# A four-layer graph network on one core: 48 tile turns per pair moved from TensorE to VectorE and DRAM

## The chip, the core and the metric

The kernel runs on one core of one Trainium2 chip. The metric is the device time of one launch in microseconds (us). Before the change the median of 3 runs is 3835.46 us (3834.73 to 3838.8); the profiled execution spans 3831.4 us. The engines that matter are TensorE (PE, with its weight loads shown apart as PEld), VectorE (DVE), ScalarE (ACT), GpSimd (POOL), and SyncE (SP), from whose single queue every transfer is issued.

## What is computed

64 graphs of 256 nodes with 256 features pass four layers. Every layer normalises its input, applies a relu, runs a graph operator and adds the result to `x`:

```
h = max(layernorm(x), 0)
layer 0: x += 8-head masked attention(h) @ Wo + bo
layer 1: x += elu(masked additive attention(h), softmax over the first node axis)
layer 2: x += gated graph network(h), 3 steps:
             m = h @ weight[i];  aggr = A^T m;  h = GRU(aggr, h)
layer 3: x += 4-head masked additive attention(h)
```

Everything is float32 but the masks.

## The kernel before, in words

**Tiling.** Two graphs make a pair: 512 tokens, four tiles of 128 tokens, in one SBUF tile of 128 partitions x 1024 floats. There are 32 pairs and every pair passes the four layers. A product on TensorE contracts over partitions, so a weight product needs the normalised tile with features on partitions: `hT`, which holds for each of two feature chunks `k` the 512 tokens side by side. The tile with tokens on partitions (`xn`, and `h` in layer 2) serves where the contraction is over nodes.

**Norm and turn.** `norm_relu_T` (L487) takes the statistics on VectorE (L494, L496), the reciprocal root on GpSimd (L504, L505), and normalises on VectorE (L526; in layer 2 on ScalarE with the relu, L521). Then TensorE turns the tile in 8 transposes of 128x128 (L541), two groups of four, each into one PSUM bank; ScalarE or VectorE evicts each bank, with the relu (L550, L551) or plain (`evict`, L315, L316).

**Layer 2.** Each of the first two GRU steps ends with the new state `u` with features on partitions. The next `messages` product (L914) needs it with tokens on partitions, so 8 further transposes (L1002) and two evictions turn it back. The gate products are at L933; the last step multiplies with the tokens on the output partitions (`tokens_mm`, L1022).

So there are six places per pair where TensorE turns a whole tile: four norms and two GRU steps, 48 transposes.

**The other way to turn, already there for the attention.** The softmax tiles of layers 0 and 3 are turned without TensorE (`turn_blocks`, L603): VectorE transposes 32x32 blocks in place (`STREAM_TRANSPOSE`, L606), one transfer writes the tile to a DRAM buffer `turn` (L608), four transfers of 32 partitions each read it back with the blocks exchanged (L611). This is done 12 times per pair. `by_dma` (L483) tells whether a norm or a GRU step is to be turned in this way too (`turn_chunks`, L621); before, it returns False always.

**Who uses a turned tile.** As stationary operand (through `chunk`, L558, or `chunk_of`, L900): the value product of layer 0 (L572), the products of layers 1 and 3 (L805, L1104), the messages (L914) and the last GRU step (L1022). As moving operand (through `wide`, L563): the query and key products (L679) and the gates (L933).

**Order.** Nothing is left to a scheduler at run time. `Plan` holds every task with an assumed duration, and `order` (L105) emits, one after another, the task that can begin first by these assumptions, with a priority from the pair's number, the length of the chain behind it and constants per layer and engine. Buffers are slots of a pool: a pair holds an `x` slot from its load to its store, working tiles are `w4` slots. Each engine then runs its instructions in this fixed order; an instruction that waits holds up all behind it on its engine, and on SyncE's queue.

Of the kernel before, what the change touches and what calls it, by code (L numbers as in the profile page):

```python
# [9 lines left out]
FP = mybir.dt.float32  # L10
# [12 lines left out]
class Buf:  # L23


    def __init__(self, tag, tiles):
        self.tag, self.tiles, self.slot, self.parts = tag, tiles, None, {}
        self.mixed = False

    def __call__(self):  # L30
# [7 lines left out]
class Plan:  # L38
# [11 lines left out]

    SPARE, GRAIN = 4, 0.01
    PERIOD, REST = 19.2988, 1.08912
    ON_PE = (170.952, 98.272, 202.056, -376.605)
    ON_SP = (-190.335, 1171.95, -256.975, 557.209)
    OTHERS = (254.735, -170.603, -1234.56, 1614.77)

    def __init__(self, slots, spare):
        self.slots, self.spare = slots, spare  # L60
# [120 lines left out]
def tile_adj_preln_d4(  # L181
# [38 lines left out]
    const = ctx.enter_context(tc.tile_pool(name="const", bufs=1))  # L220

    SLOTS = {
        "x": (5, [P, T * D], FP, 0),
        "w4": (29, [P, T * D], FP, 9),
        "f3": (2, [P, T, E3], FP, 0),
        "mask": (4, [P, T * N], BF, 1),
        "ps": (8, [P, 512], FP, 2),
# [254 lines left out]

    def by_dma(what, p):  # L483

        return False

    def norm_relu_T(xt, p, tokens=False):  # L487

        st, mv, rs = buf("st"), buf("mv"), buf("rs")
        for g in range(2):  # L490

            def stats(g=g):
                for t in (2 * g, 2 * g + 1):
# [12 lines left out]

        add((G, 1.4, rstd, True), reads=[mv], writes=[(rs, 0)])
        xn, mixed = w4(), by_dma(plan.layer, p)
        relu = tokens or mixed
        if relu:  # L510
            add(
                (V, 0.17, lambda: nc.vector.scalar_tensor_tensor(
                    rs()[:, 1, :], mv()[:, :, 0], -1.0, rs()[:, 0, :], ALU.mult, ALU.mult)),
                reads=[mv, (rs, 0)], writes=[(rs, 1)],
            )
        for g in range(2):

            def scaled(g=g):
                for t in (2 * g, 2 * g + 1):
                    if relu:  # L520
                        nc.scalar.activation(  # L521
                            tok(xn())[:, t, :], tok(xt())[:, t, :], AF.Relu,
                            bias=rs()[:, 1, t : t + 1], scale=rs()[:, 0, t : t + 1],
                        )
                    else:
                        nc.vector.tensor_scalar(  # L526
                            tok(xn())[:, t, :], tok(xt())[:, t, :], mv()[:, t, 0:1], rs()[:, 0, t : t + 1],
                            ALU.subtract, ALU.mult,
                        )

            add((A, 0.95, scaled) if relu else (V, 0.7, scaled, True), reads=[(xt, g), mv, rs], writes=[(xn, g)])
        hT = w4()
        if mixed:
            turn_chunks(xn, hT)
            return (at, hT, xn) if tokens else (at, hT)
        for k in range(2):
            ps = bank()

            def turn(k=k, ps=ps):
                for t in range(T):  # L540
                    nc.tensor.transpose(ps()[:, t * P : (t + 1) * P], tok(xn())[:, t, k * P : (k + 1) * P], ident)  # L541

            add((PE, 4 * TURN, turn), reads=[xn], writes=[ps], claims=[hT])
            dst = lambda k=k: tok(hT(), N2)[:, k, :]
            if tokens:
                add(evict(N2, dst, ps), reads=[ps], writes=[(hT, k)])
            else:
                add(
                    [
                        (A, act(N2), lambda dst=dst, ps=ps: nc.scalar.activation(dst(), ps(), AF.Relu)),  # L550
                        (V, dve(N2), lambda dst=dst, ps=ps: nc.vector.tensor_scalar_max(dst(), ps(), 0.0)),  # L551
                    ],
                    reads=[ps], writes=[(hT, k)],
                )
        return (at, hT, xn) if tokens else (at, hT)


    def chunk(hT, k, t):  # L558
        if hT.mixed:
            return hT().rearrange("p (n x) -> p x n", x=2 * T)[:, 2 * t + k]  # L560
        return tok(hT(), N2)[:, k, t * P : (t + 1) * P]

    def wide(hT, k):  # L563
        if hT.mixed:
            return hT().rearrange("p (n t k) -> p k t n", t=T, k=2)[:, k]
        return tok(tok(hT(), N2)[:, k, :], P)

    def graph_mm(ps, src, rhs, g, ):

# [33 lines left out]
    def turn_blocks(e, src, dst, eT):  # L603

        d = buf("turn")
        add((V, dve(T * N), lambda: nc.vector.transpose(dst(), src())), **e)  # L606
        e = e["writes"][0]
        add((SP, 0.6, lambda: nc.sync.dma_start(d(), e())), reads=[e], writes=[d], latency=4.6)  # L608
        for b in range(4):
            add(  # L610
                (SP, 0.55, lambda b=b: nc.sync.dma_start(  # L611
                    eT()[32 * b : 32 * b + 32, :].rearrange("p (a w) -> p a w", a=4),
                    d()[:, b * N : (b + 1) * N].rearrange("(a j) w -> j a w", a=4))),
                reads=[d], writes=[(eT, b)], latency=3.8,
            )

    def turn(e, eT):
        blocks = lambda: e().rearrange("p (r c i) -> p r c i", c=2, i=32)
        turn_blocks(dict(writes=[e]), blocks, blocks, eT)

    def turn_chunks(src, dst):  # L621

        e = w4()
        turn_blocks(
            dict(reads=[src], writes=[e]),
            lambda: src().rearrange("p (x b j) -> p b x j", b=4, j=32),
            lambda: e().rearrange("p (b i x) -> p b x i", b=4, i=32), dst,
        )
        dst.mixed = True

    def by_block(ap):
# [29 lines left out]
    def layer0(xt, p):  # L661
# [11 lines left out]
        for w, dst, nm in ((wq_sb, qT, "q"), (wk_sb, kT, "k")):  # L673
            for o in range(2):
                ps = bank()

                def product(w=w, o=o, ps=ps):
                    for k in range(2):
                        mm(ps(), w[:, k, o * P : (o + 1) * P], wide(hT, k), start=k == 0, stop=k == 1)  # L679

                add((PE, 1.72, product), reads=[hT, (QKV, int(w is wk_sb))], writes=[ps], claims=[dst])
                add(evict(N2, lambda dst=dst, o=o: tok(dst(), N2)[:, o, :], ps), reads=[ps], writes=[(dst, o)])
        for g in range(2):
            ps = bank()
            add((PE, 1.74, lambda ps=ps, g=g: graph_mm(ps, hT, wv_sb, g)), reads=[hT, (QKV, 2)], writes=[ps], claims=[v])
            add(evict(N2, lambda g=g: v()[:, g * N2 : (g + 1) * N2], ps), reads=[ps], writes=[(v, g)])


# [102 lines left out]
    def layer1(xt, p):  # L791
# [8 lines left out]
        for t in range(T):  # L800
# [6 lines left out]
            add((PE, 0.89, product), reads=[hT, W1], writes=[ps], claims=[wh, f12])  # L807
            add(
                (V, 0.07, lambda t=t, ps=ps: nc.vector.tensor_copy(f12()[:, :, t], ps()[:, D : D + 2])),
                reads=[ps], writes=[(f12, t)],  # L810
# [79 lines left out]
    def layer2(xt, p):  # L890
# [4 lines left out]
            reads=[hT], writes=[am],  # L895
        )
        at_o = lambda b, o: tok(b(), N2)[:, o, :]
        by_chunk = lambda b, o: tok(at_o(b, o), P)

        def chunk_of(h, t, o):  # L900
            if h.mixed:
# [2 lines left out]

        def messages(h):
            aT = w4()
            for o in range(2):
                ps = bank()

                def product(o=o, ps=ps):  # L910
                    for g in range(2):
                        for c in range(2):
                            t = 2 * g + c
                            mm(  # L914
                                ps()[:, g * N : (g + 1) * N], chunk_of(h, t, o), tok(am(), N)[:, t, :],
                                start=c == 0, stop=c == 1,
                            )

                add((PE, 1.73, product), reads=[h, am], writes=[ps], claims=[aT])
                add(evict(N2, lambda o=o: at_o(aT, o), ps), reads=[ps], writes=[(aT, o)])  # L920
            return aT

        for l in range(NL - 1):
            r, hn, u = w4(), w4(), w4()

            def gate(us, terms, c0, o, claims=()):
                ps = bank()
# [30 lines left out]
            for o in range(2):  # L958
# [8 lines left out]
                    writes=[(hn, o)],  # L967
                )
                add(
                    either(lambda eng, o=o, u=u, hT=hT, hn=hn: eng.tensor_sub(by_chunk(u, o), wide(hT, o), by_chunk(hn, o))),  # L970
                    reads=[(hT, o), (hn, o)], writes=[(u, o)],
                )

# [120 lines left out]
    def layer3(xt, p):  # L1094
# [4 lines left out]
        for t in range(T):  # L1099
# [6 lines left out]
            add((PE, 0.89, product), reads=[hT, W3], writes=[ps], claims=[f])  # L1106
# [125 lines left out]
```

## Time and profile before

| | before |
|---|---|
| time, median of 3 | 3835.46 us |
| span profiled, granted TensorE clock | 3831.4 us, 0.993 |
| tile turns on TensorE: L541, L1002 | 1024 and 512 instructions, 136.9 and 66.7 us busy |
| tile turns on VectorE: L606 | 384 instructions, 461.0 us busy |
| turn writes and reads by DMA | 384 of 512 KB, 1536 of 128 KB |
| DMA in all | 554.29 MB, mean 145 GB/s |

A profile row gives line, engine, operation, output<-inputs with buffer numbers left out, the shapes and the count; then the busy time of the group in us and the mean of one instruction in ns; then the idle time of the engine just before these instructions. One float32 product of the code is two PE records, except for a transpose, which is one. Matmuls overlap in the records, so a record's mean is longer than the distance from one start to the next; where the text speaks of a slot, it means this distance.

### The profile page before, as it was taken

What the parts mean: (1) busy time and instruction counts of PE and PEld (TensorE: products, weight loads), DVE (VectorE), ACT (ScalarE), POOL (GpSimd) and SP (SyncE); (2) the same over time, 40 slices, a digit from 0 to 9 for tenths busy, and PEclk for the clock granted to TensorE, in tenths of its full rate; (3) what the DMA queues carried; (4) which work ended last, traced back from release to release, by engine and by line L of the source; (5) the groups of instructions that cost most, each with busy time, mean ns of one, the idle gap of its engine ahead of it and who ended that gap; (6) DMA issues with size and microseconds to landing.
All of it is one profiled execution on the core that took longest, in us unless ns stands there. A gap on an engine that the chain in (4) does not pass through costs nothing. (4 is left out here: it accounts for less than half of the span.)

```text
span 3831.4 us, 55718 instructions
## 1 busy us (share of the span) xinstructions
PE 3771.1 (98%) x17072; PEld 2275.7 (59%) x17072; DVE 2909.2 (76%) x8279; ACT 2203.8 (58%) x6082; POOL 614.4 (16%) x595
## 2 busy tenths in 40 slices
PE   8999999999999999999999999999999999999995
PEld 5666556565666556565656565566666565655653
DVE  8796778778777788677787777786777787787655
ACT  6674456566555666555665556665456665466434
POOL 2001112111111111111111111111111111110111
PEclk9999999999999999999999999999999999999997
DMA  8354425553345544355533455442556334554224
GB/s 249 120 186 126 124 86 179 168 162 118 124 151 162 175 152 133 90 177 168 174 121 119 145 163 174 152 146 84 168 168 179 128 122 137 163 168 152 83 66 127
DMA packets 402202, 554.29 MB, mean 145 GB/s; under 512 B 40304, under 2 KB 340208, under 8 KB 401904
## 3 DMA queue, kind: packets, MB, share of 16 engines
q1 hardware_dynamic: 401904, 550.73, 46.7%
q8 instruction: 137, 2.24, 0.2%
q14 instruction: 161, 1.32, 0.1%
HBM read 332.15 MB, written 218.43 MB: 144 GB/s over the span
## 5 line engine op out<-in xcount | busy, mean ns | idle before, releaser
L655 ACT ACTIVATE w<-w,mx 128x256 f32<-128x256 f32 x1536 | 757.4, 497 | 36.7 <-DVE mx L647 36.6
L315 ACT COPY w<-ps 128x512 f32<-128x512 f32 (+1 forms) x632 | 360.8, 584 | 637.7 <-PE ps L914 165.9
L933 PE MATMUL ps<-w,giT 128*128 128x512 f32 x1536 | 712.6, 594 | 0.0
L933 PE MATMUL ps<-w,whhT 128*128 128x512 f32 x1536 | 707.9, 596 | 0.0
L933 PEld LDWEIGHTS ps<-w,giT 128*128 128x128 f32 x1536 | 288.1, 190 | 354.9 <-issue 339.0
L933 PEld LDWEIGHTS ps<-w,whhT 128*128 128x128 f32 x1536 | 283.7, 190 | 315.6 <-issue 288.2
L606 DVE STREAM_TRANSPOSE w<-w 128x1024 f32<-128x1024 f32 x384 | 461.0, 1223 | 10.3 <-ACT w L655 9.1
L647 DVE CUSTOM_DVE_ANT_0 w<-ps,mask 128x256 f32<-128x256 f32 x1024 | 368.6, 419 | 96.2 <-PE ps L699 95.0
L1022 PE MATMUL ps<-whhT,w 128*128 128x512 f32 (+1 forms) x1024 | 364.3, 489 | 0.0
L1022 PE MATMUL ps<-giT,w 128*128 128x256 f32 (+1 forms) x1024 | 359.6, 486 | 0.0
L914 PE MATMUL ps<-w,w 128*128 128x256 f32 x1536 | 355.8, 381 | 0.0
L970 POOL TENSOR_TENSOR w<-w,w 128x512 f32<-128x512 f32 x128 | 166.7, 1303 | 1114.7 <-ACT w L965 948.3
L914 PEld LDWEIGHTS ps<-w,w 128*128 128x128 f32 x1536 | 287.6, 190 | 52.3 <-issue 9.1
L655 ACT ACTIVATION_READ_ACCUMULATOR w<-w,mx 128x1 f32 x1536 | 292.2, 190 | 0.0
L1022 PEld LDWEIGHTS ps<-giT,w 128*128 128x128 f32 x1024 | 192.6, 190 | 142.0 <-issue 128.1
L1022 PEld LDWEIGHTS ps<-whhT,w 128*128 128x128 f32 x1024 | 186.9, 190 | 110.1 <-issue 96.5
L504 POOL TENSOR_SCALAR rs<-mv 128x4 f32<-128x4 f32 x128 | 37.4, 292 | 1336.9 <-DVE mv L496 1313.3
L945 ACT ACTIVATE w<-ps,brz 128x512 f32<-128x512 f32 x128 | 87.4, 683 | 239.1 <-PE ps L933 200.1
L1125 ACT ACTIVATE w<-w,f 128x256 f32<-128x256 f32 x512 | 215.4, 504 | 8.0 <-DMA w<-row 6.1
L730 DVE TENSOR_SCALAR w<-w,rz 128x256 f32<-128x256 f32 x688 | 202.4, 355 | 0.1
L494 DVE BATCH_NORM_STATS2 st<-x 128x6 f32<-128x256 f32 x512 | 189.3, 411 | 9.2 <-DMA x<-in_x_dram 7.2
L526 DVE TENSOR_SCALAR w<-x,mv,rs 128x256 f32<-128x256 f32 x384 | 155.3, 461 | 53.9 <-POOL rs L505 33.4
(119 smaller groups left out, 5750.0 us busy)
## 6 DMA issues: line engine op xcount, KB each, us to landing
turn<-w SPq DMA_DIRECT2D x384, 512.0 KB
w<-turn SPq DMA_DIRECT2D x1536, 128.0 KB
w<-in_adj_dram SPq DMA_DIRECT2D x128, 512.0 KB
w<-row SPq DMA_DIRECT2D x64, 512.0 KB
x<-in_x_dram SPq DMA_DIRECT2D x64, 256.0 KB
out_dram<-x SPq DMA_DIRECT2D x64, 256.0 KB
w<-row SPq DMA_DIRECT2D x32, 256.0 KB
w<-in_L_gnn_weight_dram SPq DMA_DIRECT2D x3, 256.0 KB
```

The costliest lines, as they stand in the source:

```text
L315: (A, act(n), lambda: nc.scalar.copy(dst(), src())),
L494: nc.vector.bn_stats(st()[:, t, :], tok(xt())[:, t, :])
L526: nc.vector.tensor_scalar(tok(xn())[:, t, :], tok(xt())[:, t, :], mv()[:, t, 0:1], rs()[:, 0, t : t + 1], ALU.subtract, ALU.mult,)
L606: add((V, dve(T * N), lambda: nc.vector.transpose(dst(), src())), **e)
L647: nc.vector.tensor_tensor_reduce(row, src, mask, scale, 3.0e38, ALU.add, ALU.min, mn)
L655: nc.scalar.activation(row, row, AF.Exp, bias=mn()[:, r : r + 1], scale=-1.0, accum_out=zs()[:, z0(r) : z0(r) + 1])
L730: op(row, row, rz()[:, r : r + 1])
L914: mm(ps()[:, g * N : (g + 1) * N], chunk_of(h, t, o), tok(am(), N)[:, t, :], start=c == 0, stop=c == 1,)
L933: mm(ps(), w[:, k, c0 : c0 + P], wide(src, k), start=n == 0, stop=n == 2 * len(terms) - 1)
L970: either(lambda eng, o=o, u=u, hT=hT, hn=hn: eng.tensor_sub(by_chunk(u, o), wide(hT, o), by_chunk(hn, o))),
L1022: mm(out, chunk(src, k, t), w[:, k, c0 : c0 + n], start=m == 0, stop=m == 2 * len(terms) - 1)
L1125: (A, act(N, 1), lambda t=t, g=g, h=h, e=e, r=r: nc.scalar.activation(rows_of(e())[:, r].rearrange("p b (c j) -> p c b j", c=2), sd[g]().r ...
```

## The change

The change takes tile turns off TensorE. `by_dma` becomes true for pairs 1 to 30; the first and the last pair turn on TensorE as before. In these 30 pairs all six turns go over VectorE and DRAM. For each turn the normalising runs on ScalarE with the relu (`relu` is true where `mixed` is), and the 8 transposes and 2 evictions are replaced by two block transposes of 512 columns each, one write of 512 KB and four reads of 128 KB.

A tile turned this way is not laid out by chunk and token. Its free axis is (node, chunk, tile of tokens): for a fixed node `n` lie 4 floats of chunk 0 and 4 floats of chunk 1 (of the four token tiles) side by side, 8 floats in all. A moving operand therefore reads runs of 4 floats with 4 skipped; a stationary operand, which needs 128 nodes of one token tile, reads single floats 8 apart. Products that take the tile as moving operand put their columns out by (node, tile), so the query and key evictions (`by_node`) sort them back on writing. In layer 2 the state stays in that order (`woven`): the messages are evicted into it, and the last step reads its stationary operands 4 floats apart.

`x` gets 6 slots for 5, so six pairs can be in flight, and `w4` 28 for 29. The constants of the planner's priorities are new, so the order of the whole program is another one.

```diff
-    SPARE, GRAIN = 4, 0.01
-    PERIOD, REST = 19.2988, 1.08912
+    SPARE, GRAIN = 4, 0.001
+    PERIOD, REST = 138.279, 1.02081
...
-        "x": (5, [P, T * D], FP, 0),
-        "w4": (29, [P, T * D], FP, 9),
+        "x": (6, [P, T * D], FP, 0),
+        "w4": (28, [P, T * D], FP, 9),
...
     def by_dma(what, p):
 
-        return False
+        return 0 < p < B // 2 - 1
...
         if hT.mixed:
-            return hT().rearrange("p (n x) -> p x n", x=2 * T)[:, 2 * t + k]
+            return hT().rearrange("p (n x) -> p x n", x=2 * T)[:, T * k + t]
+        if hT.woven:
+            return tok(hT(), N2)[:, k].rearrange("p (n t) -> p t n", t=T)[:, t]
         return tok(hT(), N2)[:, k, t * P : (t + 1) * P]
 
     def wide(hT, k):
+
         if hT.mixed:
-            return hT().rearrange("p (n t k) -> p k t n", t=T, k=2)[:, k]
-        return tok(tok(hT(), N2)[:, k, :], P)
+            return hT().rearrange("p (n k t) -> p k n t", k=2, t=T)[:, k]
+        return tok(hT(), N2)[:, k]
...
-    def turn_chunks(src, dst):
+        add((V, dve(T * N), lambda: nc.vector.transpose(blocks(), blocks())), writes=[e])
+        through_dram(e, eT)
+
+    def turn_chunks(src, order, dst):
 
         e = w4()
-        turn_blocks(
-            dict(reads=[src], writes=[e]),
-            lambda: src().rearrange("p (x b j) -> p b x j", b=4, j=32),
-            lambda: e().rearrange("p (b i x) -> p b x i", b=4, i=32), dst,
-        )
+
+        def blocks():
+            for k in range(2):
+                nc.vector.transpose(
+                    e().rearrange("p (b i k t) -> p k b t i", b=4, i=32, k=2)[:, k],
+                    src().rearrange(f"p {order} -> p k b t j", b=4, j=32, k=2)[:, k],
+                )
+
+        add((V, 2 * dve(N2), blocks), reads=[src], writes=[e])
+        through_dram(e, dst)
         dst.mixed = True
...
+                by_node = lambda ap, hT=hT: ap.rearrange("p (t n) -> p n t", t=T) if hT.mixed else ap
...
+        def messages_out(aT, o):
+            return at_o(aT, o).rearrange("p (n t) -> p t n", t=T) if woven else at_o(aT, o)
...
             if by_dma((2, l), p):
-                turn_chunks(u, h)
+                turn_chunks(u, "(k b j t)", h)
                 continue
```

More of the change, by code (lines that the diff above doesn't have):

```diff
@@ L27, in __init__ @@
         self.tag, self.tiles, self.slot, self.parts = tag, tiles, None, {}
+        self.woven = False
         self.mixed = False
@@ L48 @@
     SAME = {"PE": 0.0, "DVE": 0.1, "ACT": 0.1, "POOL": 0.1, "SP": 0.0}
-    SPARE, GRAIN = 4, 0.01
-    PERIOD, REST = 19.2988, 1.08912
-    ON_PE = (170.952, 98.272, 202.056, -376.605)
-    ON_SP = (-190.335, 1171.95, -256.975, 557.209)
-    OTHERS = (254.735, -170.603, -1234.56, 1614.77)
+    SPARE, GRAIN = 4, 0.001
+    PERIOD, REST = 138.279, 1.02081
+    ON_PE = (-212.355, -45.5106, 229.667, -1085.75)
+    ON_SP = (1007.6, 146.333, -62.4427, 928.914)
+    OTHERS = (294.968, 127.685, -2183.49, 1293.66)
     def __init__(self, slots, spare):
@@ L533, in norm_relu_T @@
         if mixed:
-            turn_chunks(xn, hT)
+            turn_chunks(xn, "(t k b j)", hT)
             return (at, hT, xn) if tokens else (at, hT)
@@ L601, in turned_keys, with through_dram @@
         return ap.rearrange("p (a t h c i) -> p h c t a i", a=4, t=2, h=2, c=2)[:, h, c]
-    def turn_blocks(e, src, dst, eT):
+    def through_dram(e, eT):
         d = buf("turn")
-        add((V, dve(T * N), lambda: nc.vector.transpose(dst(), src())), **e)
-        e = e["writes"][0]
         add((SP, 0.6, lambda: nc.sync.dma_start(d(), e())), reads=[e], writes=[d], latency=4.6)
@@ L618, in turn @@
         blocks = lambda: e().rearrange("p (r c i) -> p r c i", c=2, i=32)
-        turn_blocks(dict(writes=[e]), blocks, blocks, eT)
-    def turn_chunks(src, dst):
+        add((V, dve(T * N), lambda: nc.vector.transpose(blocks(), blocks())), writes=[e])
+        through_dram(e, eT)
+    def turn_chunks(src, order, dst):
         e = w4()
-        turn_blocks(
-            dict(reads=[src], writes=[e]),
-            lambda: src().rearrange("p (x b j) -> p b x j", b=4, j=32),
-            lambda: e().rearrange("p (b i x) -> p b x i", b=4, i=32), dst,
-        )
+        def blocks():
[6 more added lines that the diff above has]
+        through_dram(e, dst)
         dst.mixed = True
@@ L681, in layer0 @@
                 add((PE, 1.72, product), reads=[hT, (QKV, int(w is wk_sb))], writes=[ps], claims=[dst])
-                add(evict(N2, lambda dst=dst, o=o: tok(dst(), N2)[:, o, :], ps), reads=[ps], writes=[(dst, o)])
+                by_node = lambda ap, hT=hT: ap.rearrange("p (t n) -> p n t", t=T) if hT.mixed else ap
+                add(
+                    evict(
+                        N2, lambda dst=dst, o=o, f=by_node: f(tok(dst(), N2)[:, o, :]),
+                        lambda ps=ps, hT=hT: tok(ps(), T) if hT.mixed else ps(),
+                    ),
+                    reads=[ps], writes=[(dst, o)],
+                )
         for g in range(2):
             ps = bank()
-            add((PE, 1.74, lambda ps=ps, g=g: graph_mm(ps, hT, wv_sb, g)), reads=[hT, (QKV, 2)], writes=[ps], claims=[v])
+            add((PE, 2.0 if hT.mixed else 1.74, lambda ps=ps, g=g: graph_mm(ps, hT, wv_sb, g)), reads=[hT, (QKV, 2)], writes=[ps], claims=[v])
             add(evict(N2, lambda g=g: v()[:, g * N2 : (g + 1) * N2], ps), reads=[ps], writes=[(v, g)])
@@ L805, in product @@
                     mm(ps()[:, 0 : D + 2], chunk(hT, k, t), w1a[:, k, :], start=k == 0, stop=k == 1)
-            add((PE, 0.89, product), reads=[hT, W1], writes=[ps], claims=[wh, f12])
+            add((PE, 0.96 if hT.mixed else 0.89, product), reads=[hT, W1], writes=[ps], claims=[wh, f12])
             add(
@@ L897, in layer2 @@
         at_o = lambda b, o: tok(b(), N2)[:, o, :]
-        by_chunk = lambda b, o: tok(at_o(b, o), P)
+        woven = hT.mixed
+        def messages_out(aT, o):
+            return at_o(aT, o).rearrange("p (n t) -> p t n", t=T) if woven else at_o(aT, o)
         def chunk_of(h, t, o):
@@ L906, in messages @@
             aT = w4()
+            aT.woven = woven
             for o in range(2):
@@ L917, in product @@
                             )
-                add((PE, 1.73, product), reads=[h, am], writes=[ps], claims=[aT])
-                add(evict(N2, lambda o=o: at_o(aT, o), ps), reads=[ps], writes=[(aT, o)])
+                add((PE, 1.9 if h.mixed else 1.76, product), reads=[h, am], writes=[ps], claims=[aT])
+                add(
+                    evict(N2, lambda o=o: messages_out(aT, o), lambda ps=ps: tok(ps(), P) if woven else ps()),
+                    reads=[ps], writes=[(aT, o)],
+                )
             return aT
@@ L924, in layer2 @@
             r, hn, u = w4(), w4(), w4()
+            u.woven = woven
             def gate(us, terms, c0, o, claims=()):
@@ L969, in layer2 @@
                 add(
-                    either(lambda eng, o=o, u=u, hT=hT, hn=hn: eng.tensor_sub(by_chunk(u, o), wide(hT, o), by_chunk(hn, o))),
+                    either(lambda eng, o=o, u=u, hT=hT, hn=hn: eng.tensor_sub(
+                        *((tok(at_o(u, o), T), wide(hT, o), tok(at_o(hn, o), T)) if hT.mixed else (at_o(u, o), wide(hT, o), at_o(hn, o))))),
                     reads=[(hT, o), (hn, o)], writes=[(u, o)],
@@ L1104, in product @@
                     mm(ps()[:, 0:E3], chunk(hT, k, t), w3a[:, k, :], start=k == 0, stop=k == 1)
-            add((PE, 0.89, product), reads=[hT, W3], writes=[ps], claims=[f])
+            add((PE, 0.96 if hT.mixed else 0.9, product), reads=[hT, W3], writes=[ps], claims=[f])
             add(
```

## The prediction, made before the changed kernel was run

> **What bounds the kernel now.** I read the page's busy shares first, then the same by stretches of time, then the order of matmuls in a short window to get slots, then the groups.
>
> ```profile
> PE 3771.1 (98%) x17072; PEld 2275.7 (59%) x17072; DVE 2909.2 (76%) x8279; ACT 2203.8 (58%) x6082; POOL 614.4 (16%) x595
> ...
> DMA  8354425553345544355533455442556334554224
> ```
>
> TensorE is busy 98% of the span; no other engine is above 76%. A busy PE need not be a limit, so I ask where it is idle. The busy times by stretch (columns: stretch; length, then busy us and count of PE, PEld, DVE, ACT, POOL; clock, DMA share, GB/s):
>
> ```profile
> 0.00:40.00 40.00, 25.58 (x141) 17.82 (x142) 32.92 (x131) 19.68 (x56) 15.08 (x22) 0.92 0.87 281
> 40.00:115.00 75.00, 75.00 (x433) 45.74 (x433) 67.38 (x231) 53.10 (x171) 6.54 (x6) 0.98 0.78 229
> ...
> 1500.00:2000.00 500.00, 499.74 (x2225) 299.94 (x2224) 388.72 (x1116) 302.08 (x845) 79.14 (x76) 1.00 0.48 149
> ...
> 3500.00:3790.00 290.00, 278.88 (x1078) 165.06 (x1076) 184.33 (x416) 123.10 (x308) 45.56 (x39) 0.98 0.36 110
> 3790.00:3831.40 41.40, 9.33 (x40) 4.45 (x40) 14.34 (x42) 15.53 (x50) 0.00 (x0) 0.56 0.44 140
> ```
>
> In the middle PE never stops. All its idle time, 3831.4 - 3771.1 = 60 us, lies at the ends: 14.4 in the first 40 us, 43 after 3500. So from 115 to some 3600 us each nanosecond of PE taken away or added moves the end, as long as the others keep up. The order of matmuls in a window gives the slots:
>
> ```profile
> 1512.07 1.04 PE L1002 MATMUL ps<-ident,w 128*128 128x128 f32 x8
> 1512.95 1.89 PE L1022 MATMUL ps<-whhT,w 128*128 128x256 f32 x8
> 1514.67 3.62 PE L914 MATMUL ps<-w,w 128*128 128x256 f32 x16
> 1518.13 1.89 PE L1022 MATMUL ps<-whhT,w 128*128 128x256 f32 x8
> 1519.86 1.04 PE L1002 MATMUL ps<-ident,w 128*128 128x128 f32 x8
> 1520.73 1.88 PE L1022 MATMUL ps<-whhT,w 128*128 128x512 f32 x4
> 1522.45 1.88 PE L1022 MATMUL ps<-giT,w 128*128 128x512 f32 x4
> ```
>
> From one first column to the next: 8 transposes take 0.88 us, 110 ns each; a record with 256 moving columns 3.46/16 = 216 ns; one with 512, 1.72/4 = 430 ns. The weight loads lie under these. Their groups tell what a load costs:
>
> ```profile
> L914 PEld LDWEIGHTS ps<-w,w 128*128 128x128 f32 x1536 | 287.6, 190 | 52.3 <-issue 9.1 <-ACT w L1055 3.7 <-DVE mx L647 0.4
> L1147 PEld LDWEIGHTS ps<-w,f 128*64 128x64 f32 x1024 | 70.8, 141 | 95.7 <-DMA w<-turn 31.3 <-issue 30.7 <-DVE w L526 6.1
> L774 PEld LDWEIGHTS ps<-ident,f 128*4 128x4 f32 x32 | 2.7, 84 | 3.2 <-issue 0.8 <-DVE f L809 0.7 <-DVE w L987 0.2
> L606 DVE STREAM_TRANSPOSE w<-w 128x1024 f32<-128x1024 f32 x384 | 461.0, 1223 | 10.3 <-ACT w L655 9.1 <-ACT w L730 0.4
> ```
>
> 4, 64 and 128 columns take 84, 141 and 190 ns: some 81 ns that do not grow, and 0.85 ns a column, 107 ns for 128. All contiguous columns; no row shows a load or a matmul with gaps between its elements.
>
> [...]
>
> **The change part by part.**
>
> 1. Removed from PE: 8 transposes x 6 places x 30 pairs = 1440. Their starts lie 114 ns apart on average at L541 and 109 at L1002 (all between 115 and 3600 us): 960 x 0.1136 + 480 x 0.1093 = **-161 us**, all on the bound engine.
>
> 2. Added to PE by stationary operands with gaps. Records with 256 columns moving, so little cover: value product 480, layers 1 and 3 480 each, second and third messages 960, together 2400 with floats 32 bytes apart; in the last GRU step 960 more, 16 bytes apart. Another 960 there have 512 columns moving: 430 ns cover any load considered here. Low end: nothing. [...]I take half rate: 2 x 107 = 214 ns for the load, just the length of the 216 ns slot; then load and matmul run neck and neck and only imperfect overlap shows. High end: the unchanging 81 ns no longer hide, a slot of 214 + 81 = 295, +79 ns. I take +15 ns: 3360 x 0.015 = **+50 us** (0 to 265).
>
> 3. Moving operands with runs of 4 (query, key, and in the first GRU step the state's gates): 1200 records of 512. Taken as free[...].
>
> 4. Off PE, per the instruction counts of both programs. DVE: +360 transposes of 512 columns at about 0.61 us (half of 1223 ns), +220; -360 normalisings (155.3/384 = 0.404), -146; 90 more of L512's small ones, +15; small shifts of who evicts and divides, about -20: +69, to 2978 us. ACT: -363 evictions at about 0.57, -207, +360 normalisings at 0.519, +187: about 2180. POOL: 40 final sums more at 1.58: 677. Evictions that write sorted (128x128x4, 128x4x128) may cost more; even doubled, the 213 on ACT add some 120 us. None comes near the span: DVE would stand at 80%. Hidden.
>
> 5. DMA: 180 turns x 1.05 MB = 189 MB on top of 551. At today's use of the engines (46.7% of 3831 us for 551 MB) this is 613 us more: (1789 + 613)/3745 = 64%. SP issues 180 x (0.34 + 4 x 0.43) = 371 us more, spread over the run; hidden as long as it is on time.
>
> 6. The added wait. A turn was 8 transposes and two evictions of about 0.6 us; it becomes a way over DVE, two transfers and SP's queue. From the semaphore updates in the trace between 115 and 3600 us, a turn write lands 4.1 us (median; 6.0 for the slowest tenth) after its issue and a read 4.2 (5.0). Between 30 and 100 us, with the DMA engines at about 80%, medians are 3.0 and 3.9, so 64% is no cause for alarm by itself. In a GRU step the chain is tanh 0.68, two VectorE steps 1.5, transposes 1.2, write 4.1, three further issues 1.3, last read 4.2, and some hops (the chain of waits has 0.02 to 0.14 between an end and the next start): 14 us. Behind the waiting messages product stand all later matmuls. But the new order puts other pairs' work between: weighed with the slots above, 18.6 us of PE work at least and 23 in the middle for messages, 20 and 46 for layer 1, 28 and 63 for layer 3. So the margin in layer 2 is 4 to 9 us, for queueing on ACT, DVE and SP. I allow 0.3 us for each of some 60 such hops: **+20 us** (0 to 90).
>
> 7. The sixth x slot pays for the longer way of a pair (its PE work is now spread over some 620 us of PE work, 555 before) and costs nothing itself. The ends: pairs 0 and 31 are as before, but at the end pair 30 has little beside it to hide its DRAM turns, and early pairs add turns to a start where DMA is 87% busy: idle 65 us for 60.
>
> Sum: 3771 - 161 + 50 + 20 + 65 = **3745 us**, 2.4% less.
>
> **Rivals.**
>
> *Free gaps:* neither parts 2 nor 6 shows: 3771 - 161 + 60 = 3670 to 3700. For it: half-rate loads still fit the slot, and PE ran 3485 us without a gap under the same kind of order. Against it: loads at 214 ns leave no slack at all.
>
> *Late turns:* chains of 14 us meet a DVE at 80% and a loaded queue, and the fixed order passes a delay on. 0.5 us for each of 180 turns gives +90 for +20: 3815; at 1 us each, 3905. For it: a 4 us margin against a slowest tenth of 6 us at the write. Against it: the attention's 384 turns go this way now with hardly a PE wait: 37.7 us at weight loads, 27.5 of it one wait at the very end.
>
> *Loads become the bound (slower):* a load with gaps costs more than half rate, say +65 ns a record: 3360 x 0.065 = 218 for 50; 3771 - 161 + 218 + 20 + 65 = 3913. For it: no row shows one[...]. Against it: up to twice the time fits under the matmul.
>
> **How the numbers follow.** Likeliest case 0.62, at 3745. Free gaps 0.11. Late turns 0.14, of which 0.09 is still faster than before. Loads bound 0.13, nearly all of it slower. Faster 0.62 + 0.11 + 0.09 = 0.82; within 0.2% 0.03; slower 0.15. The range takes in most of the free case and of the mild late turns: 3685 to 3830.
>
> **What would show it.** Right: L541 and L1002 with 64 and 32 instructions; PE busy near 3690 with the middle stretches still full; L572 (value), L805, L1104 and L914 rows with starts 10 to 30 ns further apart, and LDWEIGHTS means near 300 for 190; gate rows unchanged; DMA share about 64%. Wrong: PE idle in the middle behind "DMA w<-turn" at the messages or the norm's products (late turns); 256-column slots above 260 ns (loads bound); gate or query rows longer than 430 ns (part 3); block transposes far above 0.6 us, with DVE near 90%.

## The result, and the profile after

The changed kernel takes 3816.5 us (3811.39 to 3820.12) beside 3836.1 us before: ratio 0.9947 (95% interval 0.9930 to 0.9964). It is faster, but by 20 us where I forecast 91. On another chip, beside later experiments, the ratio was 0.9950 (0.9935 to 0.9965).

The busy shares and the DMA row of the page after:

```profile
PE 3703.2 (97%) x15632; PEld 2423.5 (64%) x15632; DVE 3140.9 (82%) x8350; ACT 2282.9 (60%) x6061; POOL 687.5 (18%) x635
...
DMA  8766574666765757567576666666676676665434
```

PE lost 68 us of busy time, not 111; DVE gained 232, not 69; the span shrank by less than PE's busy time did, so PE now idles more: 3809.6 - 3703.2 = 106 us for 60. The busy times by stretch show where (columns as before: stretch, length, busy us and count of PE, PEld, DVE, ACT, POOL; clock, DMA share, GB/s):

```profile
40.00:115.00 75.00, 68.41 (x388) 42.98 (x389) 68.81 (x232) 56.73 (x174) 8.76 (x10) 0.95 0.79 247
...
500.00:1000.00 500.00, 495.11 (x2097) 321.04 (x2090) 416.33 (x1108) 302.85 (x816) 89.82 (x82) 1.00 0.63 194
1000.00:1500.00 500.00, 482.55 (x1977) 314.67 (x1977) 404.94 (x1068) 298.87 (x780) 89.32 (x82) 0.98 0.63 195
1500.00:2000.00 500.00, 490.24 (x2041) 317.86 (x2040) 410.23 (x1067) 301.73 (x793) 94.67 (x88) 1.00 0.67 204
...
2500.00:3000.00 500.00, 500.00 (x2161) 329.99 (x2161) 435.34 (x1172) 308.69 (x810) 99.49 (x92) 1.00 0.66 206
```

Before, the middle was full everywhere. Now PE has gaps up to 2500 us, most between 1000 and 1500, and none between 2500 and 3000: with the same work per pair, the same DMA share and an even busier DVE. The start of a layer-1 product (L863 before, L878 after) recurs every 116.7 us in pairs 22 to 28 before, every 113.35 after, a gain of 3.35 us a pair, which would be 100 us on 30 pairs. Between pairs 8 and 22 it is 117.0 before and 118.1 after. So the forecast gain is there in the last third and is lost in the first two.

What PE waits for in the middle (waits for PE between 115 and 3500 us; us in total, times, longest), the four largest after:

```profile
PE ps L687 <- DMA w<-turn: 6.7, 3, 3.0
PE ps L1172 <- DMA w<-turn: 5.9, 4, 3.2
PE ps L1129 <- DMA w<-turn: 5.4, 6, 2.1
PE ps L764 <- DMA w<-turn: 5.1, 5, 2.5
```

Before, PE waits in this stretch for a turned tile at one product alone, three times, 1.5 us in all:

```profile
L749 PE MATMUL ps<-w,w 128*32 128x256 f32 x2048 | 126.8, 382 | 1.6 <-DMA w<-turn 1.5
```

After, it waits for them at several places. L687 is the query and key product of layer 0 and L1129 the first product of layer 3; both use tiles that the change turns. L1172 and L764 (L1147 and L749 before) use the attention's softmax tiles, which went over DRAM before the change as well: their way is the same, yet PE stands idle before them for 11.0 us, for 1.5 before. The messages product, which I had singled out, comes after these four with 2.3 us. The whole list has 38 us of idle time, for 2 before. The groups that the change moved, after:

```profile
L934 PEld LDWEIGHTS ps<-w,w 128*128 128x128 f32 x1536 | 346.8, 280 | 52.5 <-issue 26.0 <-DVE w L1097 2.2 <-DVE w L909 1.2
L820 PEld LDWEIGHTS ps<-w1a,w 128*128 128x128 f32 x512 | 125.0, 325 | 7.7 <-issue 3.9
L630 DVE STREAM_TRANSPOSE w<-w 128x512 f32<-128x512 f32 x360 | 374.4, 1110 | 39.3 <-ACT w L522 36.6 <-DMA w<-turn 1.9
L316 ACT COPY w<-ps 128x512 f32<-128x512 f32 x398 | 335.2, 849 | 353.8 <-PE ps L687 86.2 <-PE ps L934 83.6 <-PE ps L764 82.0
```

A weight load with floats 32 bytes apart takes 334 ns in the median for 190 (the means here mix in the contiguous ones). A block transpose of 512 takes 1110 ns, not the 610 that I had taken. The evictions' mean rose from 585 to 849 because those that sort take 1.03 to 1.15 us. In the order of matmuls,

```profile
2537.05 2.08 PE L934 MATMUL ps<-w,w 128*128 128x256 f32 x8
2538.96 3.60 PE L957 MATMUL ps<-w,whhT 128*128 128x512 f32 x8
```

8 messages records take 1.91 us, 239 ns each for 216.

For the comparisons below I split the whole span of PE. A record's slot is the distance to the next start; what it exceeds the median of its kind by 60 ns or more counts as wait, with the time before the first matmul added. Products that use a part of the array start almost together (four of them 7 ns apart at L714 and L764, two at L1172) and are taken as one group; how they are grouped moves the sums by up to 8 us (with every unbroken run as one group the waits are 122 and 190, in the middle 47 and 107).

| | slots | waits | of these in 115 to 3500 us |
|---|---|---|---|
| before | 3711.5 | 119.9 | 45.5 |
| after | 3627.8 | 181.8 | 100.0 |
| difference | -83.7 | +61.9 | +54.5 |

The difference in slots: transposes -159.4, products with gapped stationary operands +65.7 (messages 21.6, value 10.6, layer 1 9.5, layer 3 7.8, last GRU step 16.2), all others +10.0, about as much as the grouping can move. The 512-column records with runs of 4 in the moving operand stand at 429 ns as before.

### The profile page after: what moved, and what is told of

It is laid out like the page before. It is cut to its first block, busy times and chain, and to the rows that moved or that the text cites. A ratio compares the mean times of both kernels' runs of the same rounds, so it can differ in the third digit from the quotient of the medians.

```text
span 3809.6 us, 54273 instructions
## 1 busy us (share of the span) xinstructions
PE 3703.2 (97%) x15632; PEld 2423.5 (64%) x15632; DVE 3140.9 (82%) x8350; ACT 2282.9 (60%) x6061; POOL 687.5 (18%) x635
## 5 line engine op out<-in xcount | busy, mean ns | idle before, releaser
L316 ACT COPY w<-ps 128x512 f32<-128x512 f32 x400 | 335.9, 846 | 353.8 <-PE ps L687 86.2
L621 DVE STREAM_TRANSPOSE w<-w 128x1024 f32<-128x1024 f32 x384 | 460.9, 1223 | 9.4 <-ACT w L663 7.1
L630 DVE STREAM_TRANSPOSE w<-w 128x512 f32<-128x512 f32 x360 | 374.4, 1110 | 39.3 <-ACT w L522 36.6
L934 PE MATMUL ps<-w,w 128*128 128x256 f32 x1536 | 381.0, 398 | 2.9 <-DMA w<-turn 2.3
L934 PEld LDWEIGHTS ps<-w,w 128*128 128x128 f32 x1536 | 346.8, 280 | 52.5 <-issue 26.0
L1047 PE MATMUL ps<-giT,w 128*128 128x512 f32 (+1 forms) x1024 | 364.0, 495 | 0.6 <-ACT w L316 0.6
L522 ACT ACTIVATE w<-x,rs 128x256 f32<-128x256 f32 x488 | 254.1, 589 | 163.5 <-DVE rs L513 144.3
L1047 PEld LDWEIGHTS ps<-giT,w 128*128 128x128 f32 x1024 | 276.1, 310 | 73.2 <-issue 8.5
L1047 PEld LDWEIGHTS ps<-whhT,w 128*128 128x128 f32 x1024 | 274.0, 311 | 70.8 <-issue 12.2
L1102 POOL TENSOR_TENSOR w<-w,w 128x512 f32<-128x512 f32 x64 | 101.7, 1594 | 1051.8 <-DMA w<-turn 477.2
L994 POOL TENSOR_TENSOR w<-w,w 128x512 f32<-128x512 f32 x128 | 178.7, 1402 | 461.2 <-ACT w L989 406.1
L655 DVE CUSTOM_DVE_ANT_0 w<-w,mask 128x256 f32<-128x256 f32 x512 | 192.5, 421 | 20.5 <-ACT w L1150 20.5
```

Of the source, the lines that this page charges most:

```text
L316: (A, act(n), lambda: nc.scalar.copy(dst(), src())),
L522: nc.scalar.activation(tok(xn())[:, t, :], tok(xt())[:, t, :], AF.Relu, bias=rs()[:, 1, t : t + 1], scale=rs()[:, 0, t : t + 1],)
L621: add((V, dve(T * N), lambda: nc.vector.transpose(blocks(), blocks())), writes=[e])
L630: nc.vector.transpose(e().rearrange("p (b i k t) -> p k b t i", b=4, i=32, k=2)[:, k], src().rearrange(f"p {order} -> p k b t j", b=4, j=3 ...
L655: nc.vector.tensor_tensor_reduce(row, src, mask, scale, 3.0e38, ALU.add, ALU.min, mn)
L934: mm(ps()[:, g * N : (g + 1) * N], chunk_of(h, t, o), tok(am(), N)[:, t, :], start=c == 0, stop=c == 1,)
```

## The experiments

What has to be explained is +62 us of waits (I had allowed 25) and +66 us of gapped products (50). Theory A: the gapped writes on VectorE and ScalarE, about twice as long as the planner and I assumed, make the turns late. Theory B: the way over DRAM and SyncE's queue is late by itself.

In the first four runs TensorE, VectorE, ScalarE and SyncE run the same instructions in the same order as in the changed kernel, one by one through the whole trace. Only the places differ that an instruction reads or writes, so later products see wrong data.

### Gapped stationary operands made contiguous

```diff
-            return hT().rearrange("p (n x) -> p x n", x=2 * T)[:, T * k + t]
-        if hT.woven:
-            return tok(hT(), N2)[:, k].rearrange("p (n t) -> p t n", t=T)[:, t]
+            return tok(hT(), N2)[:, k, t * P : (t + 1) * P]
...
-                return h().rearrange("p (m x) -> p x m", x=2 * T)[:, T * o + t]
+                return h().rearrange("p (x m) -> p x m", x=2 * T)[:, T * o + t]
```

> The changed kernel, but every stationary operand that is read with gaps (value product, layers 1 and 3, messages, last GRU step) reads 128 floats side by side of the same tile instead. These products get wrong data; instructions, order, buffers and waits stay. Changed kernel: span 3809.6 us, 3360 records at 233 to 240 ns. If TensorE is still what sets the end, 216 ns slots give back 3360 x about 20 ns = 66 us: 3745 to 3755. If engines behind it have become the limit (VectorE at 82%), the slots fall to 216 all the same but the time moves by less than half of it: above 3785. Weight loads back to 190 ns in either case.

Measured: 3759.3 us, ratio 0.9814 (0.9799 to 0.9828), some 52 us below the changed kernel. The weight load of the messages is back:

```profile
L932 PEld LDWEIGHTS ps<-w,w 128*128 128x128 f32 x1536 | 289.2, 191 | 80.0 <-issue 34.3 <-DVE rz L736 2.1 <-DVE w L907 1.2
```

Slots fall by 62 us, waits rise by 9 (168.5 to 177.4, without the time before the first matmul); the time is 4 us above the expected 3755. TensorE is still what sets the end, in spite of its gaps, and the gaps between the weights cost 62 us of its slots.

### Block transposes that write contiguously

```diff
-                    e().rearrange("p (b i k t) -> p k b t i", b=4, i=32, k=2)[:, k],
+                    e().rearrange("p (k b t i) -> p k b t i", b=4, i=32, k=2)[:, k],
```

> The changed kernel, but the 360 block transposes of the new turns write 512 floats side by side instead of single floats 8 apart; the tile is then sorted wrongly, so the products after it see shuffled data. Reads stay: runs of 32 for the norms, single floats 4 apart for the GRU states. Theory A (gapped writes on VectorE and ScalarE make the turns late): transposes 1.1 -> 0.61 us where the write was the cause, VectorE loses some 120 to 180 us of work, TensorE's waits in the middle fall by a good half of the 45 us that came new, time about 3780. Theory B (the way over DRAM and SyncE's queue is what makes them late): transposes shorter, time within 8 us of the changed kernel. If the gapped reads cost too, the GRU turns stay at 1.1 us.

Measured: 3796.5 us, ratio 0.9906 (0.9891 to 0.9920), some 16 us below the changed kernel; waits 155.4 for 168.5.

```profile
L630 DVE STREAM_TRANSPOSE w<-w 128x512 f32<-128x512 f32 x360 | 281.6, 821 | 39.0 <-ACT w L522 36.2 <-DMA w<-turn 1.3 <-DMA w<-in_adj_dram 0.2
```

The mean of 821 ns hides two kinds: the norms' transposes, which read runs of 32, take 0.66 to 0.73 us, and the GRU states', a third of them, which read floats 16 bytes apart, still 1.04 to 1.15. In the changed kernel, which writes with gaps, the norms' take 1.07 to 1.14 and the GRU states', with gaps on both sides, 1.08 to 1.18. So here a gap on one side made a transpose some 1.6 times as long, and one on both sides hardly longer than that. 16 us are twice the 8 of theory B; theory A's 3780 was not reached.

### Evictions that do not sort

```diff
-                        N2, lambda dst=dst, o=o, f=by_node: f(tok(dst(), N2)[:, o, :]),
-                        lambda ps=ps, hT=hT: tok(ps(), T) if hT.mixed else ps(),
+                        N2, lambda dst=dst, o=o: tok(dst(), N2)[:, o, :], ps,
...
-                    evict(N2, lambda o=o: messages_out(aT, o), lambda ps=ps: tok(ps(), P) if woven else ps()),
+                    evict(N2, lambda o=o: at_o(aT, o), ps),
```

> The changed kernel, but the evictions of query, key and messages write 512 floats side by side instead of sorting to another order of nodes; attention and gates see shuffled data. These 300 evictions then take 0.58 (ScalarE) and 0.68 us (VectorE) instead of 1.05 to 1.10. Theory A: about 140 us of ScalarE and VectorE work fall away, and some 10 to 25 us of TensorE's waits with it: 3785 to 3800. Theory B: within 8 us of the changed kernel.

Measured: 3795.8 us, ratio 0.9903 (0.9889 to 0.9918), again some 16 us; waits 154.6. ScalarE's evictions are back at the old mean:

```profile
L316 ACT COPY w<-ps 128x512 f32<-128x512 f32 x398 | 229.9, 581 | 397.7 <-PE ps L933 102.3 <-PE ps L687 101.8 <-PE ps L763 77.3
```

The time lies in theory A's range (3785 to 3800). ScalarE was at 60% and VectorE at 82%: accesses on engines that are not full cost 16 us here, as theory A has it.

### All three, and contiguous reads of the transposes

> All three at once, and the block transposes read side by side as well: no gapped access is left but the moving operands, every other instruction, the order, the transfers and the waits stay, and the data are shuffled. Theory A: slots as before the change and hardly a new wait: 3831 - 161 and up to 20 for waits and ends, 3670 to 3700, which was my case of free gaps. Theory B: the 45 us of new waits in the middle stay: 3720 to 3745.

Measured: 3718.4 us, ratio 0.9703 (0.9687 to 0.9720). Slots 3559.8, waits 141.6 for 168.5. By stretches:

```profile
1000.00:1500.00 500.00, 482.63 (x2049) 280.79 (x2047) 392.56 (x1092) 290.85 (x796) 93.09 (x86) 0.99 0.65 200
2500.00:3000.00 500.00, 499.58 (x2158) 295.04 (x2157) 417.64 (x1185) 303.98 (x848) 95.11 (x86) 1.00 0.67 210
```

Theory A alone is refuted: the time is 18 us above its range (3670 to 3700) and 2 below theory B's (3720 to 3745). Waits are 27 us below the changed kernel's, and 36 below those of the run with contiguous weights, from which this one differs by the accesses off PE alone; in time that is 41 us. 31 us of waits more than before stay, and they stay at the same place, between 1000 and 1500 us, while 2500 to 3000 is full. A way over DRAM that is late by itself should be late there too, so theory B does not fit either. The planned order differs between the two places. Weighing the order with the slots shows it: for a product that uses a turned tile, the work on PE between it and the last product before it that it depends on is 27, 58, 52, 35 us in layer 1 of pairs 13, 16, 17, 18, and 45 us for each of pairs 22 to 29; in layers 2 and 3 as well each pair from 22 to 25 is like the one before. There the order repeats. Hence theory C, so far only argued: the waits belong to an order that has not settled and that leaves no room where a turn comes later than planned.

### Planner with true durations, the old constants

```diff
-        add((V, 2 * dve(N2), blocks), reads=[src], writes=[e])
+        add((V, 2.1, blocks), reads=[src], writes=[e])
...
-            (A, act(n), lambda: nc.scalar.copy(dst(), src())),
-            (V, dve(n), lambda: nc.vector.tensor_copy(dst(), src())),
+            (A, 1.0 if gaps else act(n), lambda: nc.scalar.copy(dst(), src())),
+            (V, 1.0 if gaps else dve(n), lambda: nc.vector.tensor_copy(dst(), src())),
```

> The changed kernel, right output, with only the planner's assumed durations set to what its trace shows: block transposes of a turn 2.1 us for 1.2, evictions that sort 1.0 for 0.48 or 0.6, value product 1.91 for 2.0, last-step products 1.87 for 1.74. The priorities' constants stay, the order becomes another one. Theory A: part of the new waits stems from an order that was laid out for shorter turns, so with right durations 10 to 30 us of the 58 us come back: 3780 to 3800. Theory B (the waits are inherent to the longer way): within 10 us of the changed kernel's 3812.

Measured: 3825.7 us, ratio 0.9977 (0.9971 to 0.9984): slower than the changed kernel by some 11 us, and outside both expected ranges. Right durations alone do not make a better order. Waits are 183.1 and spread over all stretches, with 65 after 3500 us for 52.

### Each half of the change alone

```diff
-        return 0 < p < B // 2 - 1
+        return False
```

> The changed kernel with all tiles turned on TensorE as before: only the new constants, the finer grain and the slots (6 x, 28 w4) are left of the change. If the new order is good in itself, 3820 to 3840; if its constants fit only the kernel with the DRAM turns, TensorE gets gaps and it is slower than before: 3850 to 3980.

Measured: 3982.4 us, ratio 1.0391 (1.0375 to 1.0406), 2 us beyond the expected end. The new constants and slots are no gain by themselves; with the tiles turned on TensorE they cost 4%.

The other half, with the planner's lines and the two slot counts of the kernel before:

> The turns through DRAM alone: the changed kernel with the constants, the grain and the slots of the kernel before (5 x, 29 w4). If the sixth pair and the new order are needed to hide the longer way of a turn, TensorE waits in the middle and the gain is lost: 3870 to 3960. If they are not, within 15 us of the changed kernel, 3800 to 3825.

Measured: 4046.5 us, ratio 1.0557 (1.0541 to 1.0572), 86 us beyond the expected end. PE's waits over its whole span begin:

```profile
PE ps L1172 <- DMA w<-turn: 29.5, 5, 26.9
PE ps L934 <- DMA w<-turn: 25.1, 6, 8.1
PE ps L820 <- DMA w<-turn: 21.4, 3, 12.6
PE ps L714 <- DVE mx L655: 20.3, 3, 12.4
```

Its slots are 3646.7, and waits have grown to 384. The same turns cost 213 us or bring 20, by the order and the slot counts. Which of the two does how much was not tried apart.

### Orders with more room for the transfers

All work is as in the changed kernel, the planner's durations as in the run with true costs, and the constants were searched anew, with more or less room planned for the transfers of a turn. The lines of the run that went best (the second below):

```diff
-    PERIOD, REST = 138.279, 1.02081
-    ON_PE = (-212.355, -45.5106, 229.667, -1085.75)
-    ON_SP = (1007.6, 146.333, -62.4427, 928.914)
-    OTHERS = (294.968, 127.685, -2183.49, 1293.66)
+    PERIOD, REST = 180.471, 1.02081
+    ON_PE = (-214.097, -45.5106, 232.611, -1085.75)
+    ON_SP = (1007.6, 146.333, -22.7758, 928.914)
+    OTHERS = (294.968, 127.685, -2183.49, 1088.14)
...
-        add((SP, 0.6, lambda: nc.sync.dma_start(d(), e())), reads=[e], writes=[d], latency=4.6)
+        add((SP, 0.6, lambda: nc.sync.dma_start(d(), e())), reads=[e], writes=[d], latency=5.399)
...
-                reads=[d], writes=[(eT, b)], latency=3.8,
+                reads=[d], writes=[(eT, b)], latency=5.138,
```

> The changed kernel, right output, all turns and all gapped accesses kept. The planner has the durations of the trace (as in the run with true durations), and besides more room for the transfers of a turn (write 4.96 us for 4.6, each read 4.41 for 3.8), and constants searched so that the order ends early even when each transfer lands later than planned. Theory C (the new waits come from an order with no room where transfers land late, not from the DRAM way or the gaps as such): slots stay at 3628 us, waits of TensorE fall from 168 to 90 to 120, 3735 to 3770. Theory B (waits are inherent to the longer way): above 3795.

> As the run before, from another search, with most room for the transfers (write 5.40, read 5.14 us planned); the planner's own end is 3735.1 us. Theory C: 3740 to 3770. Theory B: above 3795.

> The counterpart: the true durations and constants searched in the same way, so that the planner's own end is 3733.6 us, but with the transfers' planned times left at 4.6 and 3.8 us. If the constants alone matter (searched or not), it is as fast as the two runs before, within 10 us. If the room for late landings matters (theory C), it is 15 to 60 us slower than they are, by waits for turned tiles in the middle.

> The changed kernel itself, once more, beside the three above for a comparison on one chip: 3812 +- 6 us.

| planned for write, read (us) | time (us) | ratio to before | slots | waits (without the first) |
|---|---|---|---|---|
| 4.6, 3.8: changed kernel again | 3813.5 | 0.9950 (0.9935 to 0.9965) | 3628.4 | 169.8 |
| 4.6, 3.8: constants searched | 3818.7 | 0.9960 (0.9947 to 0.9973) | 3630.6 | 174.6 |
| 4.96, 4.41 | 3808.1 | 0.9931 (0.9915 to 0.9948) | 3627.6 | 167.0 |
| 5.40, 5.14 | 3779.4 | 0.9858 (0.9843 to 0.9872) | 3617.6 | 142.6 |

The order with most room beats the changed kernel by 34 us and the one before by 54. Its stretches, and its only wait of PE for a turned tile between 115 and 3500 us:

```profile
500.00:1000.00 500.00, 499.94 (x2144) 329.48 (x2143) 438.36 (x1151) 314.08 (x837) 93.27 (x82) 1.00 0.67 208
1000.00:1500.00 500.00, 499.93 (x2130) 329.16 (x2129) 439.35 (x1139) 310.28 (x826) 96.19 (x87) 1.00 0.67 207
...
2500.00:3000.00 500.00, 499.93 (x2101) 330.94 (x2100) 436.88 (x1129) 315.61 (x840) 92.14 (x83) 1.00 0.67 209
```

```profile
PE ps L764 <- DMA w<-turn: 0.8, 1, 0.8
```

The order searched without more room, for comparison:

```profile
PE ps L1129 <- DMA w<-turn: 13.2, 11, 2.0
PE ps L764 <- DMA w<-turn: 9.4, 13, 2.0
```

In the best run PE is full from 500 to 3000 us, with VectorE at 88%, the DMA engines at 67%, and every gapped access still in. The waits in the middle are 65 us for 100. So neither the DRAM way nor the engines' load forces the waits: theory B falls. What is shown is that the plan alone (the order, and which engine takes an eviction), with the same products and turns, moves the time from 3826 to 3779.

Of theory C one half falls too. In the traces of all three searched orders the sequence of PE's products repeats, from the fifth or seventh pair to the last few: in the best run every four pairs, 113.9 us a pair on average; in the run with 4.96 and 4.41 every five, 115.0 us a pair; in the run without more room every two, 116.0 us a pair. All three have settled, and the last waits as much as the changed kernel. So an order that repeats is not enough.

Whether the room for late landings is what makes the difference is open. The four rows fit it, and so does the changed kernel's trace, in which a read lands 5.3 us after its issue in the slowest tenth, beyond 4.4 and near 5.1. Against my expectation the run with 4.96 and 4.41 gained only 5 us on the changed kernel, 38 us short of my range, and by itself it would have spoken for theory B (above 3795). The run without more room is 39 us behind the best one, as theory C has it, but only 11 behind the other, where 15 to 60 were expected. The best one missed its range by 9; its ends cost more than before (63 us of waits after 3500 us for 52). And each row has its own constants and its own sequence of products, so room is not isolated.

### The gapped writes once more, in the order of 3779 us

> The faster of the settled orders (3779 us), with the writes of the block transposes and of the sorting evictions side by side, as in the two runs that changed these alone in the changed kernel and gained 16 us each; products after them see shuffled data. The order, laid out for the long durations, stays. If gapped writes cost time only by making turns late in an order without room, they cost next to nothing here: 3770 to 3780. If they hold TensorE up whatever the order is, 30 us again: 3745 to 3755.

The edits are those of the runs on turn writes and on evictions, both at once. Measured: 3776.1 us, ratio 0.9849 (0.9833 to 0.9865), beside 0.9858: no difference that these runs can tell. The edits that gained 16 us each in the changed kernel's order gain nothing in this one, although VectorE loses 108 us of work by them and ScalarE 92. So the gapped writes off TensorE had no fixed price: 16 us for each of the two in one order, nothing that could be told in the other.

## Why the prediction was wrong, point by point

In the span the forecast was -161 + 50 + 20 + 5 = -86 us, and measured are -159 + 66 + 10 + 62 = -21 with rounding. Of the 64 us missed 37 are waits (part 6, and the accesses of part 4 that feed them), 16 are gapped weights (part 2) and 10 are other slots.

**What bounds the kernel** was right: TensorE before and after. 62 us off its slots gave 52 us off the time.

**Part 1, the transposes:** -161 forecast, -159 measured. (What moved are six tile turns, which are 48 transposes, in each of 30 pairs, not 48 turns.)

**Part 2, gapped stationary operands:** +50 forecast, +66 measured. That gapped loads lengthen the slot was right, the size too small: half rate, an assumption of mine that no row before showed, gave a load of 214 + 81 = 295 ns, and it takes 334. With the 81 ns taken as unchanged, I estimate (334 - 81)/128 = 2.0 ns a column for 0.85, 253 ns for 128 columns and so more than the slot of 216. The slot grew to 238 to 240 ns at 32 bytes and to 233 at 16 (where a load takes 309 ns in the median), some 20 ns more on average where I took 15. How load and slot share the time no run shows.

**Part 3, moving operands in runs of 4:** taken as free, an assumption that no row before showed; measured are 429 ns with and without gaps.

**Part 4, "Hidden":** this step failed, in size and in reasoning. I halved 1223 ns for the new transposes, although I had taken gapped loads on TensorE at half rate; they write single floats 32 bytes apart and take 1110. For the evictions I did say "even doubled", and they nearly doubled (on ScalarE from 0.58 to 1.03 to 1.15 us). But I tested only whether an engine's sum came near the span. DVE stood at 82%, and yet the gapped accesses cost 27 to 36 us of waits (and 41 us of time between the two runs with contiguous weights), because their result is waited for. In the order of 3779 us the gapped writes cost nothing that could be told. Hidden was here a matter of when, not of how much.

**Part 5, DMA:** 64% forecast, 63% measured. In the median landings did not grow longer: write 3.1 us (4.1 before), read 4.05 (4.2); the slowest tenth of the reads went from 5.0 to 5.3.

**Part 6, the added wait:** the main miss. I allowed 20 us; measured are +54 in the middle. I computed one chain, with transposes of about half their real length, and compared it with typical room at the messages, layer 1 and layer 3. Two things had no term at all. The norm of layer 0 was not in the comparison, and before its product (L687) PE stood idle longest, 6.7 us. And the attention's own turns, which I had taken as a sign that this way costs hardly a wait, held PE up for 11.0 us at L764 and L1172. The messages, tightest by my count, stand at 2.3 us. So the room of a single chain did not tell where PE would wait. The waits depend on the whole order, and another order with the same turns has 0.8 us of idle time for turned tiles in place of 25. What in an order decides it stays open.

**Part 7, the ends:** +5 us forecast; measured are +9 before 115 us and -1 after 3500. What the sixth slot does was never run apart.

**The sum and the signs.** "PE busy near 3690" does not come out of the sum, which gives 3771 - 161 + 50 = 3660; 3703 was measured. Of the signs of being wrong, PE idle behind `w<-turn` at the norms' products came, and so did block transposes far above 0.6 us, with DVE at 82% and not 90%.

**The rivals:** late turns at 0.5 us each, worked out as 3815 and given 0.14, names what happened, but that it hits the time is in part luck: it has 95 us of new waits where 62 were measured, and 50 us of gapped products where 66 were, with +10 of other slots besides. Its argument that the fixed order passes a delay on fits what was found; its DVE at 80% and its loaded queue do not, since the best order has DVE at 85% and the same transfers. The argument against it, the attention's 384 turns with hardly a wait, was weak in two ways: the 37.7 us at weight loads are those of L1147 alone (L749 had 12.5 more), and these turns' waits grew with the new order. Against the free case speaks part 2; with all gaps gone 3718 us were left, above its 3700. A better order without the gaps was not run, so whether the lower end of my range can be reached is not known.

## What to carry to other kernels

In this kernel, whose order is fixed in advance, moving work off the full engine paid what the order let it (the same turns cost 213 us or brought 20): compare the same stretch of the repeating part and of the rest before judging the change itself. Count the waits of everything that shares the way, not only of what is moved. Ask of every access that it moves to another engine whether it runs over neighbouring floats; with single floats 16 bytes or more apart, weight loads took 309 to 334 ns for 190 here, block transposes 1.04 to 1.18 us for 0.66 to 0.73, evictions 1.00 to 1.15 us for 0.58 (ScalarE) and 0.68 (VectorE). Measured durations in the plan are not enough (3826 us with them and the old constants); an order has to be searched for the work that it orders, and tried with landings later than the median. Two halves that each lost 4 to 6% alone gained 0.5% together.

## What the hardware showed that I had not expected

- A block transpose on VectorE of 128x512 floats: 0.66 to 0.73 us with both sides in runs, 1.04 to 1.15 with reads 16 bytes apart, 1.07 to 1.14 with writes 32 bytes apart, 1.08 to 1.18 with both.
- An eviction of 128x512 from PSUM that writes floats 16 or 512 bytes apart: 1.03 to 1.15 us on ScalarE (0.58 contiguous) and 1.00 to 1.14 on VectorE (0.68). The medians at 16 and at 512 bytes are 1.09 and 1.06 us on ScalarE, 1.10 and 1.05 on VectorE.
- A weight load of 128 floats 32 bytes apart: 334 ns in the median for 190, and a 256-column slot of 238 to 240 ns for 216.
- 189 MB more through the DMA engines, from 47% to 63% of their time, did not lengthen the landings of the turns in the median: 3.1 us for 4.1 at the writes, 4.05 for 4.2 at the reads.
